# Four engines instead of one in the order of the program: a transformer layer on one core of Trainium2

## The chip, the cores and the metric

The kernel runs on one core of one Trainium2 chip. Times are device microseconds of that core. Five engines work at the same time, each through its own queue of instructions: TensorE (PE in the profile; PEld is its weight load), VectorE (DVE), ScalarE (ACT), GpSimd (POOL) and SyncE (SP), which here only issues DMAs. An instruction waits on semaphores until what it reads has been written and what it overwrites has been read; the instructions behind it in the same queue wait with it.

## The reference, cut to what matters

One layer over 4096 tokens of 256 features: attention with 16 heads of 16 features and a causal mask, and a feed-forward part with hidden size 1024, each followed by a residual and a layer norm.

```python
xn  = (x - mean) * rsqrt(var + 1e-5) * gamma + beta
q, k, v = split(xn @ w_qkv.T)                 # 16 heads of 16
attn = softmax(causal(q @ k.T / 4)) @ v       # 4096 x 4096 per head
x = layernorm(x + attn)
h = silu(x @ w1.T * s1) * (x @ w2.T * s2)     # 256 -> 1024
h = gelu(h @ h1.T * s_h1)                     # 1024 -> 1024
h = gelu(h @ h2.T * s_h2)                     # 1024 -> 1024
x = layernorm(x + h @ w3.T * s3)              # 1024 -> 256
```

Everything is float32. The kernel splits operands of products into a high and a low part of a rounded kind (`fp32r`, written `FR`) and adds the products, so that a product is two or three matmuls.

## The kernel before, in words

The tokens are cut into 8 blocks of 512. Three kinds of work are woven into one stream on TensorE.

**Projections** (`projections`, a generator). For each block: load x (`xb`, SP), layer norm (`norm_steps`: statistics `st` and `mv` on VectorE, L132 and L133; `ve` and `rs` on GpSimd, L137 and L138; `mr` on VectorE, L141; four applies on ScalarE, L145), transposes and `xn` (`front`, L221 and L222), the split into `xh` and `xl` (L227, L229); then the products for keys, queries and values, each copied out of PSUM as a high and a low part (`kh` L263, `kl` L265; values `vst` L287) and written to DRAM (`kaug`, `qaug`, `vaug`). From the second block on GpSimd issues those writes. Two buffers hold `xb`, two each `kh` and `kl`.

**Attention.** Blocks of queries are taken in the order `ORDER`, four heads at a time. `row_max` forms all scores of a query block once for their row maxima: for every 128 queries and two heads a score tile of two PSUM banks (L435, with the mask added on the diagonal by `pick` and `tri`, L442), reduced by VectorE into `mp` (L446), which GpSimd has set to a large negative value before (L426). `scores` forms the scores a second time, transposed and with the maximum subtracted in the product (L479), ScalarE takes the exponential (`p`, L483), GpSimd clears what lies over the diagonal (L486, an affine select), and `product` multiplies by the values into `opsum` (L497). The score tiles of both, the projections' outputs and the small transposes share three PSUM buffers with the tag `s`; transposes and feed-forward products share one buffer with the tag `m`.

**Feed-forward** (`feed`, a generator for each block; two may be under way). Weights are loaded by GpSimd's DMA queue into three buffers a slot (`wt`, L660) while the block runs. The tanh (L789) and two combinations (L790, L792) make the gated product; L834 copies the hidden products out; `gelu` (L743) changes ScalarE's table and takes four tiles at once; GpSimd splits the results into high and low parts (`act`, L738 and L739). Two output products (L854) are scaled by VectorE (`th`, L861) and added to the residual by GpSimd (L863), followed by the layer norm with the same steps and the store.

**What sets the order.** The Python code emits instructions in one order, the order of the program. The loop in `layer` emits up to three tiles of row maxima and scores and then calls `other`, which emits a piece of projections or feed-forward work and products by the values. Small work that waits for something is put off by hand: `defer` puts a step into a lane with a delay, and `chore`, called once by each `other`, takes at most one ripe step out of the lanes. Splits after a gelu, the residual and the steps of the layer norm go through these lanes.

From that list a scheduler makes each engine's queue, by its own estimate of when an instruction is ready. For TensorE it is held to the order of the program: `in_order` adds an edge from each instruction of an engine to the engine's next one, and is called for TensorE alone. The queues of VectorE, ScalarE, GpSimd and SP are the scheduler's, with one exception: exponentials and gelus are chained to one another on ScalarE (`chain("table")`). In the projections the first block's loads and statistics stand under a high priority.

The last block's feed-forward part runs alone at the end (`self.tail`). There GpSimd has no splits, VectorE makes them, and `inspect` (L714) compares every weight tile with a second, raw copy loaded by SP, and counts differences. At the very end a branch on that count chooses a general path, which is not taken with these inputs.

Of the kernel before, what the change touches and what calls it, by code (L numbers as in the profile page):

```python
# [21 lines left out]
NB = N // B  # L22
# [21 lines left out]
def tokens(ap):  # L44
    return ap.rearrange("(t p) e -> p t e", p=P)


class Layer:
# [13 lines left out]
    @contextmanager  # L62
    def in_order(self, *engines):

        block = self.nc.cur_bb.bb
        start = len(block.instructions)
        yield
        last = {}
        for i in block.instructions[start:]:
            if i.engine in engines:  # L70
                if i.engine in last:
                    self.after(i, last[i.engine])
                last[i.engine] = i.name
# [8 lines left out]
    def run(self):  # L82
        tc, nc, a = self.tc, self.nc, self.a
        with ExitStack() as ctx:
            dram = self.pool(ctx, "dram", space=DRAM)
            cst = self.pool(ctx, "cst")
            self.small = self.pool(ctx, "small", 4)
            self.qaug = [dram.tile([H, 48, B], F32, name=f"qaug{b}") for b in range(NB)]
            self.kaug = [dram.tile([H, KR, B], F32, name=f"kaug{b}") for b in range(NB)]
            self.vaug = [dram.tile([NQ, P, 4, 4, D + 1], F32, name=f"vaug{b}") for b in range(NB)]  # L90
            self.attn = [dram.tile([B, E], F32, name=f"attn{b}") for b in range(NB)]

            self.ident = cst.tile([P, P], F32, name="ident")
            make_identity(nc, self.ident)
            self.mhalf = cst.tile([P, 4], F32, name="mhalf")
            nc.gpsimd.memset(self.mhalf, -0.5)
            self.wbad = cst.tile([P, 22], F32, name="wbad")
            self.wseq = (
                [("glu", g, 0) for g in range(4)]
                + [(n, g, k) for n in ("h1T", "h2T") for g in range(4) for k in range(2)]  # L100
                + [("w3T", 0, k) for k in range(2)]
            )
            self.sc = {}
            for n in ("w1_s", "w2_s", "h1_s", "h2_s"):
                self.sc[n] = cst.tile([P, 8], F32, name=n)
            self.w1_half = cst.tile([P, 8], F32, name="w1_half")
            self.w12 = cst.tile([P, 8], F32, name="w12")
            self.s3 = cst.tile([P, E], F32, name="s3")

            with ExitStack() as fctx, self.in_order(mybir.EngineType.PE):  # L110
                self.layer(fctx)
            bad = self.verdict(cst)
            with tc.If(bad > 0), ExitStack() as gctx:
                self.general(gctx)
# [86 lines left out]
    def projections(self, ctx):  # L201

        nc, a, ps = self.nc, self.a, self.ps
        one = self.pool(ctx, "p1", side="right")
        wk = self.pool(ctx, "pw", 2, side="right")

        def norm(b):  # L210
            xb = wk.tile([P, 4, E], F32, name="xb")
            nc.sync.dma_start(xb, tokens(a["x"][b * B : (b + 1) * B]))
            self.layernorm(xb, xb)
            return xb

        def front(b, xb):
            xn = wk.tile([P, 2, B], F32, name="xn", bufs=1)
            for c in range(2):
                tp = ps.tile([P, B], F32, name="m", tag="m")
                for t in range(4):  # L220
                    nc.tensor.transpose(tp[:, t * P : (t + 1) * P], xb[:, t, c * P : (c + 1) * P], self.ident)  # L221
                nc.scalar.activation(  # L222
                    xn[:, c], tp, AF.Identity, bias=bet[:, c : c + 1], scale=gam[:, c : c + 1]
                )
                yield 4 * TRANSPOSE, True
            xh = wk.tile([P, 2, B], FR, name="xh")
            nc.vector.tensor_copy(xh, xn)  # L227
            xl = wk.tile([P, 2, B], FR, name="xl")
            nc.vector.tensor_tensor(xl, xn, xh.bitcast(F32), ALU.subtract)  # L229
            parts[b] = xh, xl  # L230

        w = one.tile([P, 2, 3 * E], F32, name="wqkv")
        nc.scalar.dma_start(w, a["wqkvT"].rearrange("(k p) f -> p k f", p=P))
        gam = one.tile([P, 2], F32, name="gam")
        nc.scalar.dma_start(gam, a["gamma"].rearrange("(c p) -> p c", p=P))
        bet = one.tile([P, 2], F32, name="bet")
        nc.scalar.dma_start(bet, a["beta"].rearrange("(c p) -> p c", p=P))
        parts = {}
        with self.tc.high_priority():
            xb = norm(0)  # L240
            yield from front(0, xb)
        xb = norm(1)
        wh = one.tile([P, 2, 3 * E], FR, name="wh")
        nc.vector.tensor_copy(wh, w)
        wl = one.tile([P, 2, 3 * E], FR, name="wl")
        nc.vector.tensor_tensor(wl, w, wh.bitcast(F32), ALU.subtract)
        ones = one.tile([32, B], F32, name="ones")
        nc.gpsimd.memset(ones, 1.0)
        vst = [one.tile([P, NQ, 4, 4, D + 1], F32, name=f"vst{i}") for i in range(2)]
        for v in vst:  # L250
            nc.gpsimd.memset(v, 1.0)
        for b in range(NB):
            xh, xl = parts.pop(b)
            prods = [(wh, xh, c) for c in range(2)] + [(wl, xh, c) for c in range(2)] + [(wh, xl, c) for c in range(2)]
            for off, dst, order in ((E, self.kaug, (0, 0, 1)), (0, self.qaug, (0, 1, 0))):
                kp = ps.tile([P, 2, B], F32, name="s", tag="s", bufs=3)
                for T in range(2):
                    for n, (wp, xp, c) in enumerate(prods):
                        nc.tensor.matmul(
                            kp[:, T], wp[:, c, off + T * P : off + (T + 1) * P], xp[:, c], start=n == 0, stop=n == 5  # L260
                        )
                kh = wk.tile([P, 2, B], FR, name="kh")
                nc.scalar.copy(kh, kp)  # L263
                kl = wk.tile([P, 2, B], FR, name="kl")
                nc.vector.tensor_tensor(kl, kp, kh.bitcast(F32), ALU.subtract)  # L265
                for n, (i, g) in enumerate(sorted((i, g) for g, i in enumerate(order))):
                    for T in range(2):
                        queues = (nc.scalar, nc.sync, nc.gpsimd) if b == 0 else (nc.gpsimd,)
                        queues[(2 * n + T) % len(queues)].dma_start(
                            dst[b][8 * T : 8 * T + 8, 16 * g : 16 * g + 16, :], (kh, kl)[i][:, T].bitcast(F32)  # L270
                        )
                yield 12 * MM, True
                if dst is self.kaug:
                    nc.sync.dma_start(self.kaug[b][:, 48:KR, :], ones)
                    if b + 1 < NB:
                        yield from front(b + 1, xb)
                        if b + 2 < NB:
                            xb = norm(b + 2)
            v = vst[b % 2]
            vps = ps.tile([P, 4, E], F32, name="s", tag="s", bufs=3)  # L280
            for t in range(4):
                for n, (wp, xp, c) in enumerate(prods):
                    nc.tensor.matmul(
                        vps[:, t], xp[:, c, t * P : (t + 1) * P], wp[:, c, 2 * E :], start=n == 0, stop=n == 5
                    )
            for t in range(4):
                nc.scalar.copy(v[:, :, t, :, 0:D], vps[:, t].rearrange("p (q h d) -> p q h d", q=NQ, d=D))  # L287
            nc.gpsimd.dma_start(
                self.vaug[b].rearrange("q p t h d -> p q (t h d)"), v.rearrange("p q t h d -> p q (t h d)")
            )  # L290
            self.projected = b
            yield 12 * MM, True
# [702 lines left out]
```

## Time and profile before

| | |
|---|---|
| median of 3 runs | 2544.71 us (2540.38 to 2558.79) |
| profiled execution | 2547.4 us, of it 2545.2 from the first to the last instruction |
| busy: PE, DVE, ACT, POOL | 2263.3, 1540.0, 1389.4, 706.4 us |
| granted TensorE clock, mean | 0.926 |
| DMA | 310.02 MB, mean 122 GB/s |

A busy time says what an engine worked in the span; a view by windows gives the same for a stretch of it, with the granted clock. In the waits, a line reads: who waited, for whom, how long in all, how often, and the longest. In the timeline, a line reads: start, duration, engine, line of the kernel, operation, tile written from tile read, shapes, count, and in brackets the idle time of the engine just before with what ended it. "SPq" and "ACTq" are DMA issues by those queues.

### The profile page before, as it was taken

Reading aid. Unit: us, or ns where it says so; the run is one execution under the profiler, and the core shown is the slowest. Engines: PE = TensorE matmul, PEld = TensorE weight load, DVE = VectorE, ACT = ScalarE, POOL = GpSimd, SP = SyncE. Lnnn points to the kernel's source line nnn. Section 1 sums busy time; section 2 is a strip of 40 time slices with the busy share of each in tenths; the row PEclk is TensorE's granted clock in tenths of the full one; section 3 lists DMA queues with packets and bytes.
Section 4 is the critical chain, followed back from the end, with each engine's and each line's share of the span. In section 5 each row is a group of like instructions: output and inputs, shape, how many; then the busy total and the mean of one; then the engine's idle time right before and its main releaser. Section 6 shows DMA issues by size and latency. Waiting matters only on the chain. (4 is left out here: it accounts for less than half of the span.)

```text
span 2545.2 us, 36334 instructions
## 1 busy us (share of the span) xinstructions
PE 2263.3 (89%) x13986; PEld 1218.5 (48%) x13986; DVE 1540.0 (61%) x1800; ACT 1389.4 (55%) x1695; POOL 706.4 (28%) x1021
## 2 busy tenths in 40 slices
PE   4777989999998989999998989889999999999776
PEld 3555445445445545544454534444455543445355
DVE  3544777675666576676755577556766468761164
ACT  3332645555665665556655656556655667566621
POOL 3333232341323142403304041232313132221311
PEclk8887879989999989999998989999999989999989
DMA  7766644536454435444444434435353543443365
GB/s 208 203 164 178 149 108 120 118 103 128 109 119 128 117 81 118 106 118 120 110 115 106 106 94 113 114 102 136 90 124 102 126 112 88 116 111 87 94 178 154
DMA packets 251795, 310.02 MB, mean 122 GB/s; under 512 B 41312, under 2 KB 179680, under 8 KB 251616
## 3 DMA queue, kind: packets, MB, share of 16 engines
q1 hardware_dynamic: 141904, 184.87, 25.8%
q0 software_dynamic: 108352, 120.91, 21.6%
q8 instruction: 113, 1.85, 0.3%
q10 hardware_dynamic: 1360, 1.84, 0.2%
q14 instruction: 66, 0.54, 0.1%
HBM read 268.45 MB, written 38.54 MB: 121 GB/s over the span
## 5 line engine op out<-in xcount | busy, mean ns | idle before, releaser
L446 DVE TENSOR_REDUCE mp<-s 128x2 f32<-128x1024 f32 (+3 forms) x1152 | 1270.0, 1132 | 587.3 <-PE s L435 438.7
L483 ACT ACTIVATE p<-s 128x1024 f32<-128x1024 f32 (+3 forms) x1152 | 1060.5, 954 | 704.5 <-PE s L479 694.2
L479 PE MATMUL s<-qt,sk 50*128 50x512 f32 (+3 forms) x2304 | 514.4, 453 | 88.5 <-DVE mp L446 46.5
L435 PE MATMUL s<-mk,qt 48*128 48x512 f32 (+3 forms) x2304 | 515.0, 448 | 71.9 <-DVE mp L446 30.0
L497 PE MATMUL opsum<-p,vk 128*17 128x512 f32 (+3 forms) x4608 | 559.5, 587 | 11.9 <-POOL p L486 11.3
L816 PE MATMUL m<-act,wt 128*128 128x512 f32 x1792 | 480.5, 411 | 1.2 <-issue 1.1
L479 PEld LDWEIGHTS s<-qt,sk 50*128 50x128 f32 x2304 | 223.4, 193 | 403.6 <-DVE mp L446 145.5
L435 PEld LDWEIGHTS s<-mk,qt 48*128 48x128 f32 x2304 | 230.5, 197 | 326.3 <-ACT p L483 148.8
L816 PEld LDWEIGHTS m<-act,wt 128*128 128x128 f32 x1792 | 324.1, 191 | 125.7 <-issue 55.3
L497 PEld LDWEIGHTS opsum<-p,vk 128*17 128x17 f32 x4608 | 97.8, 97 | 240.0 <-issue 208.9
L486 POOL TENSOR_SCALAR_AFFINE_SELECT p<-p 128x256 f32<-128x256 f32 x256 | 102.9, 411 | 297.0 <-ACT p L483 295.6
L660 POOL DMA_DIRECT2D wt<-h2T_in x64 | 48.6, 759 | 411.7 <-PE m L816 338.6
L660 POOL DMA_DIRECT2D wt<-h1T_in x64 | 49.3, 770 | 361.8 <-PE m L816 225.5
L739 POOL TENSOR_TENSOR act<-raw,act 128x512 fp32r<-128x512 f32 x112 | 140.3, 1272 | 0.0
L834 ACT ACTIVATE raw<-m,h_s 128x512 f32<-128x512 f32 x112 | 77.1, 689 | 111.3 <-PE m L816 111.3
L786 PE MATMUL m<-xh,wt 128*128 128x512 f32 x224 | 103.9, 464 | 15.7 <-DVE th L790 14.1
L442 PEld LDWEIGHTS s<-tri,pick 64*128 64x128 f32 x1024 | 98.6, 209 | 7.1
L786 PE MATMUL m<-xl,wt 128*128 128x512 f32 x224 | 91.6, 409 | 0.0
L442 PE MATMUL s<-tri,pick 64*128 64x128 f32 (+1 forms) x1024 | 90.0, 255 | 0.0
L738 POOL CAST act<-raw 128x512 fp32r<-128x512 f32 x112 | 65.3, 610 | 54.9 <-ACT raw L743 54.9
L816 PE MATMUL bank<-act,wt 128*128 128x512 f32 x256 | 65.2, 411 | 15.2 <-DMA wt<-h2T_in 6.7
L738 POOL CAST act<-th 128x512 fp32r<-128x512 f32 x56 | 34.5, 616 | 145.7 <-DVE th L792 145.6
(118 smaller groups left out, 1480.2 us busy)
## 6 DMA issues: line engine op xcount, KB each, us to landing
mk<-kaug SPq DMA_DIRECT2D x288, 200.0 KB
sk<-kaug SPq DMA_DIRECT2D x288, 200.0 KB
wt<-h1T_in POOLq DMA_DIRECT2D x64, 512.0 KB, 4.3
wt<-h2T_in POOLq DMA_DIRECT2D x64, 512.0 KB, 4.2
vk<-vaug SPq DMA_DIRECT2D x144, 136.0 KB
qt<-qaug SPq DMA_DIRECT2D x64, 192.0 KB
wt<-w1T_in POOLq DMA_DIRECT2D x34, 256.0 KB, 4.0
wt<-w2T_in POOLq DMA_DIRECT2D x34, 256.0 KB, 4.1
```

The costliest lines, as they stand in the source:

```text
L435: nc.tensor.matmul(m[:, e, :k1], qt[rows, r, t * P : (t + 1) * P], kt[rows, r, :k1], start=True, stop=kb != qb,)
L442: nc.tensor.matmul(m[:, e, k1 - P + half * i : k1], pick[rows, i], tri[rows, : P - half * i], start=False, stop=i == 1,)
L446: nc.vector.tensor_reduce(mp[:, r, :, t, kb], m[:, :, :k1], AX.X, ALU.max)
L479: nc.tensor.matmul(s[:, e, lo:], kt[rows, r, t * P : (t + 1) * P], qt[rows, r, lo:], start=True, stop=True)
L483: nc.scalar.activation(p[:, :, lo:], s[:, :, lo:], AF.Exp, scale=0.25)
L486: nc.gpsimd.affine_select(out=p[:, :, lo : lo + P], in_=p[:, :, lo : lo + P], compare_op=ALU.is_ge, fill=0.0, base=0, pattern=[[0, 2], [1, ...
L497: nc.tensor.matmul(opsum[32 * j : 32 * j + D + 1, lo:], vt[:, t, j], pt[j // 2][:, j % 2, lo:], start=first, stop=last,)
L660: self.nc.gpsimd.dma_start(dst, src)
L738: eng.tensor_copy(hi, src)
L739: eng.tensor_tensor(lo, src, hi.bitcast(F32), ALU.subtract)
L786: nc.tensor.matmul(s, wt[:, 2 * i + k, cols], x[:, k], start=k == n == 0, stop=k == n == 1)
L816: nc.tensor.matmul(s, wts[k // 4][:, k % 4, cols], x[:, k % 4], start=k == n == 0, stop=k == 7 and n == 1)
```

## The change

The order of the program becomes binding for VectorE, ScalarE and GpSimd too; instructions that issue DMAs are left out of it on every engine, so that the scheduler still places them. In the projections, the high priority of the first block goes. The load of a block's x and its layer norm, which `norm` emitted together, are pulled apart: `fetch` emits the load at the old place, and the layer norm comes later in the program, for the second block behind the split of the weights and the fills of `ones` and `vst`, for the later blocks between the key and query products and the value product.

```diff
@@ in_order
-            if i.engine in engines:
+            if i.engine in engines and "DMA" not in type(i).__name__:
@@ run
-            with ExitStack() as fctx, self.in_order(mybir.EngineType.PE):
+            own = mybir.EngineType
+            with ExitStack() as fctx, self.in_order(own.PE, own.DVE, own.Activation, own.Pool):
                 self.layer(fctx)
@@ projections
-        def norm(b):
+        def fetch(b):
             xb = wk.tile([P, 4, E], F32, name="xb")
             nc.sync.dma_start(xb, tokens(a["x"][b * B : (b + 1) * B]))
-            self.layernorm(xb, xb)
             return xb
...
-        with self.tc.high_priority():
-            xb = norm(0)
-            yield from front(0, xb)
-        xb = norm(1)
+        xb = fetch(0)
+        ahead = fetch(1)
+        self.layernorm(xb, xb)
+        yield from front(0, xb)
+        xb = ahead
         wh = one.tile([P, 2, 3 * E], FR, name="wh")
...
         for v in vst:
             nc.gpsimd.memset(v, 1.0)
+        self.layernorm(xb, xb)
         for b in range(NB):
...
                         if b + 2 < NB:
-                            xb = norm(b + 2)
+                            xb = fetch(b + 2)
+            if b + 2 < NB:
+                self.layernorm(xb, xb)
             v = vst[b % 2]
```

Lines of the changed kernel lie up to four higher than before: the row maxima at L450, the exponentials at L487.

## The prediction

> **What bounds the kernel now.** I read the page's busy table first, then the span cut into four stages, then the waits of VectorE (DVE) and TensorE (PE), then the timeline around the longest PE gaps.
>
> ```profile
> PE 2263.3 (89%) x13986; PEld 1218.5 (48%) x13986; DVE 1540.0 (61%) x1800; ACT 1389.4 (55%) x1695; POOL 706.4 (28%) x1021
> ...
> PEclk8887879989999989999998989999999989999989
> ```
>
> ```profile
> core 0: us, PE busy (x) PEld busy (x) DVE busy (x) ACT busy (x) POOL busy (x), PEclk, DMA share, GB/s
> 0.00:60.00 60.00, 26.25 (x121) 20.84 (x121) 22.28 (x56) 20.05 (x35) 20.85 (x46) 0.87 0.73 202
> 60.00:256.00 196.00, 144.02 (x895) 103.82 (x895) 95.74 (x152) 66.12 (x119) 74.86 (x136) 0.80 0.71 186
> 256.00:2368.00 2112.00, 1964.01 (x12345) 1006.82 (x12349) 1345.69 (x1443) 1248.63 (x1473) 568.60 (x790) 0.94 0.45 112
> 2368.00:2546.00 178.00, 128.97 (x630) 87.01 (x627) 76.23 (x149) 54.60 (x69) 42.12 (x50) 0.89 0.53 145
> ```
>
> PE sets the time in the long third stage: 1964 of 2112 us busy. It is idle 34 us in the first stage, 52 in the second, 148 in the third, 49 in the last. So what the other engines' order is worth must be read from those gaps. VectorE's waits tell why they arise:
>
> ```profile
> DVE st L132 <- POOL x L863: 38.4, 13, 8.5
> DVE st L132 <- DMA xb<-x_in: 26.4, 6, 6.7
> DVE st L132 <- POOL x L679: 26.0, 5, 9.1
> ```
>
> (total, times, longest). A statistics instruction stands in VectorE's queue before its input is ready, and the row maxima behind it, which free the score buffers, wait too. One such place:
>
> ```profile
> 1361.32 1.25 POOL L863 TENSOR_TENSOR x<-x,th 128x512 f32<-128x512 f32 x1
> 1362.54 0.40 POOL L486 TENSOR_SCALAR_AFFINE_SELECT p<-p 128x256 f32<-128x256 f32 x1
> 1362.61 0.75 DVE L132 BATCH_NORM_STATS2 st<-x 128x6 f32<-128x256 f32 x2 [8.44 <-POOL x L863]
> 1363.28 2.34 DVE L446 TENSOR_REDUCE mp<-s 128x2 f32<-128x1024 f32 x2
> 1364.54 0.80 PE L479 MATMUL s<-qt,sk 50*128 50x512 f32 x2 [7.94 <-DVE mp L446]
> ```
>
> VectorE sat 8.44 us before `st` until GpSimd (POOL) had added the residual; two row maxima, long ready, followed; PE lost 7.94 us. GpSimd was late because splits of the other block filled it without a break from 1349.4 to 1361.3.
>
> **The change, stage by stage.** No matmul is added or removed, and PE's own order is the same. The sum is made against the profiled execution: 2547.4 us, span 2545.2, and it lies 2.7 above the median of 2544.7.
>
> *Third stage, 256 to 2368: statistics, splits, selects.* In the order before, two of a feed-forward block's four statistics stand 0 to 2 row maxima after each of its two output products (L861); in the changed order all four stand 5 to 12 row maxima after the second, in each of the six blocks that end beside row maxima. One maximum takes 1.22 us, so they come 6 us or more later, against blocked times of up to 8.5. Splits were issued back to back (0.61 cast and 1.27 subtraction each; from 897.8 to 907.4 without a break, and PE waited 5.03 us for the select behind them); now selects come between. PE gaps over 1.2 us that these moves explain, in order of time: 2.03, 1.86, 4.72, 5.03, 7.94, 3.31, 5.28, 7.66, 4.48, together **42.3 us**. I take all as gone.
>
> Each gap is also followed by a stretch of granted clock 0.50. Eight such stretches belong to these gaps: 17.1, 6.8, 17.1, 13.7, 20.5, 10.2, 10.2, 6.8, in all 102.4 us, in which the windows view has PE busy 72.6. Here a rule is weighed. The Trainium skill, "TensorE: Matmul & The Clock Gate", its table of terms and "HAM oscillation", prices the penalty at throttled time times one minus the granted share: 102.4 x 0.5 = 51 us. But 30 of the 102 are the gaps themselves, which I have counted; by the row 72.6 x 0.5 = 36 is the most. Half of that ran beside VectorE working off its backlog (busy 49.6 of the 102), which limits PE at any clock. I take half of 36, **18 us**. By the rule the stage's gain would be 93, by the row 79, my value 60.
>
> Against it stand new waits. ScalarE's (ACT's) tanh at L789 and VectorE's L790 behind it now stand back to back with no row maximum between; 22 of them wait 24.4 us now, 1.1 each; were all 56 to wait it, VectorE loses 62 us more or less, of which PE sees what the three score buffers don't cover. VectorE is idle 766 us of this stage, so I take a fifth, **12 us** (ends 0 and 62). The 32 `mp` memsets (0.2 us each), which ran far ahead on GpSimd, now stand where a row-maximum step begins, on average 52 places later. In the changed order 13 follow a select, 9 a split, 5 a `rs`, none directly a weight trigger (10 did before); I cost them at nothing beyond the 12, cover being the two other score buffers, some 2.3 us. Third stage: -42 - 18 + 12 = **-48 us**, ends -79 and +20.
>
> *First stage, 0 to 60.* Without `vst`'s memset (1.01 us) between `ve` and `rs`, and without `wh` and `wl` (0.93 and 1.72 us) ahead of `mr`, the first apply starts some 2.5 us earlier. Those two casts then stand behind `xl`, so the first products start at about 18.7 instead of 19.2. Block 2's `xn` no longer waits behind block 3's apply (the 9.4 us PE gap to 45.1); block 2's own apply, now behind `kl` of the first queries, ends about 38.7, which makes PE's next product some 3.4 us earlier. But `pick`, `tri`, `opsum` and the first `mp` memsets, done by 17 us before, now come after block 1's 12 POOL triggers and the third block's `ve` and `rs` (1.3 us). Those triggers end at 60.5 now, about 57 then; with 1.3 and some 2.2 of memsets and copies the first row maximum can run at about 60.5 to 61, where it runs at 61.2. I take **0**, ends -4 and +4. SP's order changes little: the feed-forward's first two x loads go ahead of the eight `ones` loads, 0.5 MB each, landing long before use.
>
> *Second stage, 60 to 256: projections beside attention.* Gone: 3.83, 4.75 and 7.49 us, where PE waited for VectorE blocked in statistics, 16 us; 27.2 us at clock 0.50 follow them with PE busy 19.4, worth up to 10, I take 7. New: in six blocks the layernorm is issued in one piece. From the first `st`, VectorE needs 2.2 us, GpSimd 1.3 (0.27 and 1.05), and ScalarE holds its exponentials until then, and for four applies (2.4) after: about 6 us, of which the V products (2.8 us) and two buffers hide all but 2: 6 x 2 = 12. About five `mp` memsets stand behind six key or query triggers (0.6 us each), 1 us each: 5. -23 + 17 = **-6 us**, ends -23 and +18, because the DMA engines are 71% busy and some gaps wait for them.
>
> *Last stage.* The comparison of weights with their raw copy (L714, 1.22 us) moves behind the split of the even chunk, where it stood ahead of the product. A weight buffer is free only when PE and this comparison are both done with it; PE needs it until 1.9 us into the odd chunk, the comparison is now done 3.4 us into it, so the next `wt` trigger comes 1.5 us later. PE already waits for those transfers:
>
> ```profile
> PE bank L816 <- DMA wt<-h2T_in: 6.7, 4, 2.0
> PE bank L816 <- DMA wt<-h1T_in: 5.1, 4, 2.1
> ```
>
> This is where a rule speaks against the change: "DMA: Bandwidth & Descriptors", its rules for kernel authors, wants a DMA issued early and its semaphore waited on late. By it the 1.5 us is paid in all eight waits, 12 us; by the row, in which the DMA engines are 83% busy from 2453 to 2526 and the bandwidth is part of the limit, it could be 0. I take **7**. The last block's residual and statistics now follow the other block's `mr`: 0.4 us more. Together +7.
>
> **Sum:** 0 - 6 - 48 + 7 = -47; 2547.4 - 47 = 2500 in a profiled execution, and 2544.7 - 47 = **2498 us** in the median.
>
> **Rivals.** About 1%, 25 us, is what a measurement of this kernel can tell from no change.
> *Deeper:* all of the clock and no new waits: -79 - 23 + 7 = -95, 2450 us. For it: the gaps and slow stretches are in the rows. Against: some 83 us of the third stage's idle is in gaps under 1.2 us, which VectorE and ScalarE at 64% and 59% leave anyway.
> *Swallowed:* in strict order VectorE and ScalarE wait for one another at each tanh, `hl`, `xl` and reciprocal, which the old order filled with maxima: the 12 becomes 50, the second stage +0: 0 + 0 - 10 + 7 = -3, about 2540. For it: `hl` and `xl` stand 2.6 and 2.8 places earlier. Against: PE consumes in the same order, so who waits, waits for what PE needs next.
> *Slower, by the `mp` memsets:* a memset caught behind a blocked weight trigger holds the row maxima. A trigger waits 7.0 us for PE (715.4 in 102), plus 0.76 and 0.2, less 2.3 of cover: 5.7 each. From 8 of 32 the gain is eaten; with 16 it is +91 - 47 = +44, 2589 us. For it: 13 stand within four places behind a trigger. Against: none directly behind one.
> That the order isn't what it says is ruled out by the two programs' orders of instructions side by side.
>
> **Chances.** Forecast 0.46 (its own range 2475 to 2519), deeper 0.15, swallowed 0.25, slower 0.14. Faster: 0.46 + 0.15 = 0.61; within 1%: 0.25; slower 0.14. Leaving out a third of deeper and most of slower gives 2452 to 2566.
>
> **What would show it.** Right: `st` waits on L863 and L679 near 0; no PE gap over 4 us between 300 and 2370; PEclk of the third stage at 0.97 or more; PE waits for `wt` in the last stage at 17 to 24 us. Wrong: VectorE's first maximum waiting for the memset by more than 2 us each; `xb` applies with long idle before them and PE idle over 52 us from 60 to 256.

## The result: 0.5% faster, a gain of 64 us beside a loss of 50

The changed kernel takes 2537.89 us (median of 20 runs, 2529.82 to 2549.54), the kernel before 2551.14 in the same series (20 runs). The ratio is 0.9947, 95% interval 0.9927 to 0.9966: 13 us faster where 47 were forecast. The profiled execution spans 2530.6 us, before 2545.2. Its page, busy time of TensorE and granted clock in 40 slices:

```profile
PE 2259.3 (89%) x13986; PEld 1218.9 (48%) x13986; DVE 1546.9 (61%) x1800; ACT 1391.5 (55%) x1695; POOL 708.4 (28%) x1021
...
PEclk8778989979998989999999999999999999999787
```

Between the 17th slice and the last three, the clock row of before has three slices at 8 (the prediction shows the row); now there is none. The last three read 787 where 989 stood. The totals hide this. Since TensorE's order is the same in both, the span can be cut where the same work has been done. I take the start of two row-maximum reductions, numbers 96 and 1151 counted from 0 among the 1184 reductions into or from `mp` (the expectations below call them the 96th and the last, though 32 more follow the second). The windows between and behind these marks, first of the changed kernel:

```profile
core 0: us, PE busy (x) PEld busy (x) DVE busy (x) ACT busy (x) POOL busy (x), PEclk, DMA share, GB/s
293.10:2191.20 1898.10, 1802.76 (x11480) 926.14 (x11473) 1285.96 (x1380) 1158.26 (x1366) 531.89 (x734) 0.96 0.46 115
2191.20:2531.00 339.80, 249.61 (x1257) 152.14 (x1253) 115.00 (x186) 126.00 (x150) 69.14 (x86) 0.85 0.40 109
```

The same work in the kernel before:

```profile
293.90:2255.50 1961.60, 1821.09 (x11480) 935.87 (x11477) 1285.17 (x1380) 1155.27 (x1363) 529.67 (x732) 0.95 0.44 111
2255.50:2546.00 290.50, 237.71 (x1257) 142.75 (x1253) 111.97 (x186) 125.97 (x150) 68.61 (x86) 0.91 0.47 127
```

The counts of TensorE (11480, 1257) agree, so the pieces may be subtracted. Up to mark 96 the kernels differ by 0.8 us, between the marks the changed one is 63.5 us shorter, and behind mark 1151 it is 49.7 us longer (339.4 to its own end against 289.8). In the middle TensorE's idle time fell from 140.5 to 95.3 us and its busy time from 1821.1 to 1802.8. At the end its idle time rose and its clock fell from 0.91 to 0.85.

VectorE's waits in the changed kernel (total, times, longest) show which waits went:

```profile
DVE mp L450 <- POOL mp L430: 21.8, 9, 4.6
...
DVE st L133 <- DMA xb<-x_in: 6.4, 1, 6.4
DVE st L133 <- POOL x L867: 1.0, 1, 1.0
```

Statistics waited 38.4 us for the residual's addition and 26.0 for the attention's; 1.0 is left of both. TensorE's waits show where the end is longer:

```profile
PE bank L820 <- DMA wt<-h1T_in: 24.8, 5, 6.4
PE bank L820 <- DMA wt<-h2T_in: 21.2, 4, 5.9
...
PE bank L858 <- DMA wt<-w3T_in: 4.7, 1, 4.7
```

Before, these weight waits were 5.1, 6.7 and 1.9 us. One pair of hidden chunks in the last stage shows how 2 us of waiting became 6. The timeline of the changed kernel (start, duration, engine, line; in brackets the idle time before):

```profile
2388.00 8.88 PE L820 MATMUL bank<-act,wt 128*128 128x512 f32 x32 [2.91 <-DMA wt<-h1T_in]
...
2391.47 0.69 ACT L832 ACTIVATE th<-bank,h_s 128x512 f32<-128x512 f32 x1 [11.14 <-PE bank L820]
2392.20 0.43 DVE L742 CAST act<-th 128x512 fp32r<-128x512 f32 x1 [3.71 <-ACT th L832]
...
2393.27 1.22 DVE L718 SCALAR_TENSOR_TENSOR raw<-raw,wt 128x1024 f32<-128x1024 f32 x1
...
2395.03 0.74 POOL L664 DMA_DIRECT2D wt<-h1T_in  x1 [5.25 <-DVE raw L718]
...
2396.18 0.74 POOL L664 DMA_DIRECT2D wt<-h1T_in  x1 [0.41 <-issue]
...
2403.29 1.22 PE L820 MATMUL bank<-act,wt 128*128 128x512 f32 x2 [6.41 <-DMA wt<-h1T_in]
```

And the same place in the kernel before:

```profile
2459.60 1.23 DVE L714 SCALAR_TENSOR_TENSOR raw<-raw,wt 128x1024 f32<-128x1024 f32 x1 [0.49 <-DMA wt<-h1T_in]
...
2459.62 7.55 PE L816 MATMUL bank<-act,wt 128*128 128x512 f32 x32 [0.95 <-DMA wt<-h1T_in]
...
2461.77 0.69 ACT L828 ACTIVATE th<-bank,h_s 128x512 f32<-128x512 f32 x1 [5.01 <-PE bank L816]
...
2463.84 0.95 POOL L660 DMA_DIRECT2D wt<-h1T_in  x1 [6.77 <-PE bank L816]
...
2465.66 0.74 POOL L660 DMA_DIRECT2D wt<-h1T_in  x1 [0.87 <-PE bank L816]
```

Before, the comparison runs the moment its weight has landed, beside TensorE's first products with it, and what frees the buffer is TensorE. In the changed kernel it stands behind the even chunk's gelu and split, and the trigger's releaser is `raw L718`. That holds for eight triggers (before, for none):

```profile
POOL wt L664 <- DVE raw L718: 90.9, 8, 14.5
```

Measured from the even chunk's gelu, the first trigger comes after 3.56 us instead of 2.07, 1.5 us later. From then to TensorE's next start 8.3 us pass instead of 5.4 (to 2469.28 in the trace of before). The copies for the comparison are set off by the same comparisons:

```profile
2394.52 0.37 SPq L717 DMA_DIRECT2D raw<-h1T_in  x1
...
2395.67 0.37 SPq L717 DMA_DIRECT2D raw<-h1T_in  x1
```

So four transfers of 0.5 MB start within 1.7 us. In the pair of before they are spread over 4.8 us (copies at 2460.86 and 2464.18). Over seven pairs of chunks (first to fifteenth gelu of the two hidden layers) a pair takes 105.56 / 7 = 15.1 us, before 68.77 / 7 = 9.8.

### The profile page after: what moved, and what is told of

Its sections match the earlier page's. It is cut to its first block, busy times and chain, and to the rows that moved or that the text cites. A ratio compares the mean times of both kernels' runs of the same rounds, so it can differ in the third digit from the quotient of the medians.

```text
span 2530.6 us, 36361 instructions
## 1 busy us (share of the span) xinstructions
PE 2259.3 (89%) x13986; PEld 1218.9 (48%) x13986; DVE 1546.9 (61%) x1800; ACT 1391.5 (55%) x1695; POOL 708.4 (28%) x1021
## 5 line engine op out<-in xcount | busy, mean ns | idle before, releaser
L450 DVE TENSOR_REDUCE mp<-s 128x2 f32<-128x1024 f32 (+3 forms) x1152 | 1264.8, 1132 | 549.3 <-PE s L439 393.3
L487 ACT ACTIVATE p<-s 128x1024 f32<-128x1024 f32 (+3 forms) x1152 | 1062.8, 954 | 664.9 <-PE s L483 648.2
L439 PE MATMUL s<-mk,qt 48*128 48x512 f32 (+3 forms) x2304 | 509.8, 444 | 56.2 <-DVE mp L450 17.8
L501 PE MATMUL opsum<-p,vk 128*17 128x512 f32 (+3 forms) x4608 | 552.6, 581 | 2.4 <-POOL p L490 1.4
L820 PE MATMUL m<-act,wt 128*128 128x512 f32 x1792 | 473.3, 406 | 0.7 <-DVE xl L773 0.7
L501 PEld LDWEIGHTS opsum<-p,vk 128*17 128x17 f32 x4608 | 97.4, 97 | 230.6 <-issue 211.4
L490 POOL TENSOR_SCALAR_AFFINE_SELECT p<-p 128x256 f32<-128x256 f32 x256 | 102.1, 408 | 286.6 <-ACT p L487 281.4
L820 PE MATMUL bank<-act,wt 128*128 128x512 f32 x256 | 76.8, 467 | 46.0 <-DMA wt<-h1T_in 24.8
L790 PE MATMUL m<-xh,wt 128*128 128x512 f32 x224 | 104.1, 465 | 12.8 <-DVE th L794 10.2
L820 PEld LDWEIGHTS bank<-act,wt 128*128 128x128 f32 x256 | 58.8, 234 | 64.1 <-DMA wt<-h1T_in 19.7
```

Source lines behind the costliest of these rows:

```text
L439: nc.tensor.matmul(m[:, e, :k1], qt[rows, r, t * P : (t + 1) * P], kt[rows, r, :k1], start=True, stop=kb != qb,)
L450: nc.vector.tensor_reduce(mp[:, r, :, t, kb], m[:, :, :k1], AX.X, ALU.max)
L487: nc.scalar.activation(p[:, :, lo:], s[:, :, lo:], AF.Exp, scale=0.25)
L490: nc.gpsimd.affine_select(out=p[:, :, lo : lo + P], in_=p[:, :, lo : lo + P], compare_op=ALU.is_ge, fill=0.0, base=0, pattern=[[0, 2], [1, ...
L501: nc.tensor.matmul(opsum[32 * j : 32 * j + D + 1, lo:], vt[:, t, j], pt[j // 2][:, j % 2, lo:], start=first, stop=last,)
L790: nc.tensor.matmul(s, wt[:, 2 * i + k, cols], x[:, k], start=k == n == 0, stop=k == n == 1)
```

## The experiments

All times by mark are of profiled executions, the medians and ratios of the runs beside the kernel before on the same chip (its median was 2548.75 to 2554.18 us in those series).

| | to mark 96 | 96 to 1151 | 1151 to end | median | ratio, interval |
|---|---|---|---|---|---|
| before | 293.9 | 1961.6 | 289.8 | 2551.14 | |
| changed | 293.1 | 1898.1 | 339.4 | 2537.89 | 0.9947 (0.9927 to 0.9966) |
| early comparison | 290.5 | 1902.0 | 293.8 | 2489.53 | 0.9804 (0.9744 to 0.9864) |
| order only | 322.1 | 1909.9 | 345.5 | 2569.95 | 1.0074 (1.0042 to 1.0105) |
| by hand only | 294.5 | 1961.4 | 288.1 | 2546.15 | 0.9991 (0.9969 to 1.0013) |
| statistics loose | 292.3 | 1910.8 | 336.5 | 2550.28 | 0.9988 (0.9966 to 1.0010) |
| GpSimd ordered | 294.4 | 1939.7 | 290.4 | 2528.20 | 0.9906 (0.9886 to 0.9925) |
| VectorE ordered | 300.2 | 1913.9 | 343.3 | 2559.21 | 1.0031 (1.0009 to 1.0053) |
| ScalarE ordered | 282.4 | 1957.3 | 289.0 | 2535.82 | 0.9938 (0.9915 to 0.9960) |
| no raw copies | 297.0 | 1898.6 | 304.7 | 2502.63 | 0.9816 (0.9759 to 0.9872) |
| VectorE, not statistics | 301.5 | 1955.8 | 339.2 | 2594.41 | 1.0167 (1.0109 to 1.0225) |
| late start | 281.4 | 1904.1 | 296.2 | 2490.14 | 0.9767 (0.9703 to 0.9831) |
| memsets loose | 301.5 | 1891.0 | 292.2 | 2477.64 | 0.9707 (0.9655 to 0.9758) |
| last stage ordered | 291.0 | 1962.6 | 342.4 | 2601.43 | 1.0212 (1.0156 to 1.0267) |

A mark is read from a single execution. Three of the kernels have the same program up to the last stage (changed, early comparison, no raw copies); they reach mark 96 at 290.5 to 297.0 us and take 1898.1 to 1902.0 between the marks. So differences of some 7 us in the first column and 4 us in the second can be chance.

**Early comparison.** The changed kernel with the comparisons of a pair emitted ahead of the even chunk's gelu and split.

```diff
                 if self.tail:
-                    if c % 2:
+                    if c % 2 == 0:
                         for k in range(2):
                             self.inspect(g + k, wts[k])
```

> The changed kernel with one edit in the last stage: the two weight comparisons of a pair of chunks (L718) are emitted ahead of the even chunk's gelu and split instead of behind it. Theory A (late comparisons hold the weight buffers, so the weight transfers and the copies for the comparison all start together at the end of a pair and DMA idles before): the pair of chunks, 15.4 us long in the changed kernel, goes back to about 9.3 us, PE's waits for wt from 51 to about 15 us, half clock in the last stage from 70.7 to about 45; all in all 2538 - 48 = 2490 us, ratio to before 0.975 to 0.979. Rival B (the order of POOL's triggers or bandwidth sets the pair's length): pairs stay at 14 us or more, and the time within 8 us of 2538, ratio 0.993 to 0.997.

Measured: 2489.53 us. The last stage falls from 339.4 to 293.8 us and a pair to 9.1. TensorE's waits for weights:

```profile
PE bank L820 <- DMA wt<-h1T_in: 11.4, 6, 3.6
PE bank L820 <- DMA wt<-h2T_in: 4.6, 4, 1.7
```

Theory A holds: one move of two instructions carries nearly all of the loss, and without it the order gives 2%. What is left of the loss is a wait of TensorE for the last comparison, 4.6 us, which this edit does not move.

**Last stage ordered.** The reverse: the kernel before, with VectorE's order binding only behind the point where the last block's feed-forward begins.

```diff
         self.tail = True
+        self.mark = len(nc.cur_bb.bb.instructions)
@@ in_order
-        for i in block.instructions[start:]:
-            if i.engine in engines:
+        dve = mybir.EngineType.DVE
+        for n, i in enumerate(block.instructions):
+            if n < (self.mark if i.engine == dve else start):
+                continue
+            if i.engine in engines + (dve,):
```

> The kernel before with one part of the change alone: VectorE's order binding in the last stage only, nothing else. Theory A (the place of the comparisons is the whole loss there): up to the last row maximum as before, the last stage 40 to 52 us longer, in all 2591 to 2604 us, ratio 1.016 to 1.021. Rival B (the loss needs GpSimd's or ScalarE's order as well): within 12 us of before.

Measured: 2601.43 us, the last stage 52.6 longer (just above the range) and the rest within 3. Theory A again, this time without any other part of the change.

**No raw copies.** What makes the landing long? The changed kernel without the loads of the raw copies, the comparison reading the weight tile twice.

```diff
-        for dst, src in self.sources(j, raw):
-            nc.sync.dma_start(dst, src)
         nc.vector.scalar_tensor_tensor(
-            raw, raw, 1.0, wt.bitcast(F32), ...
+            raw, wt.bitcast(F32), 1.0, wt.bitcast(F32), ...
```

> The changed kernel without the loads of the raw weight copies in the last stage (L717); the comparison reads the weight tile against itself, with the same VectorE work at the same place, so that no difference could be found. A pair of chunks took 15.4 us in the changed kernel, 9.25 before: the trigger of a weight load comes 2.7 us later after the pair's start, and trigger to landing takes 8.1 instead of 5.0 us. Theory A (the copies, set off at the same moment by the same comparison, make the landing long): landing at 5 us or less, a pair at 10.5 to 12.5 us, the last stage 25 to 40 us shorter, in all 2498 to 2513 us, ratio 0.979 to 0.985. Rival B (weights landing late only through the late trigger and the slower clock): landing at 7 us or more, a pair at 14 us or more, in all 2528 or more.

Measured: 2502.63 us, a pair at 72.34 / 7 = 10.3 us, just under the range. From the tile view of the weights' triggers, in the changed kernel (last stage):

```profile
DMA to landing us min/median/max: 4.1/8.0/8.7
```

and here:

```profile
DMA to landing us min/median/max: 3.3/4.1/5.4
```

(before: median 5.0). Theory A holds. With the comparison at its late place but no copies beside the weights, 34.7 of the 49.7 us are gone. In the changed kernel the DMA engines were busy 53% of the time from 2370 to 2500, in the kernel before 76% from 2437 to 2526: they waited, and then had two pairs of transfers at once. The amount alone is not the cause: the early comparison moves the same copies, and its weights land after a median of 5.0 us. From 2397 to 2403 us the trace of the changed kernel has packets of both queues, 929 of the weights' and 630 of the copies'. This agrees with the Trainium skill, "DMA: Bandwidth & Descriptors", section "Queues, rings and completion order", which says that a DMA engine takes turns between its queues packet by packet. Then a weight and a copy started together can both land late. The trace does not show the turns of a single DMA engine.

**Order only** and **by hand only.** The two parts of the change, each alone.

```diff
 order only: the kernel before, with
+            if i.engine in engines and "DMA" not in type(i).__name__:
+            with ExitStack() as fctx, self.in_order(own.PE, own.DVE, own.Activation, own.Pool):
 by hand only: the changed kernel, with
+            with ExitStack() as fctx, self.in_order(own.PE):
```

> The kernel before with the binding order for the four engines, without the placement by hand in the projections. Theory A (the order alone makes the third stage's gain, 64 us from 300 to 2310, and the last stage's loss of 50; the placement by hand repairs what the order would cost in the projections): third stage 60 to 70 us shorter than before, last stage 45 to 55 longer, and the time up to the 96th row maximum 10 to 30 us later than in the changed kernel, in all 2548 to 2568 us, ratio 0.999 to 1.007. Rival B (the placement is of no use, or part of the third stage's gain is its): up to the 96th maximum no later than the changed kernel, in all 2530 to 2545, ratio under 0.998, or a third stage that gains under 40 us.

> The placement by hand in the projections alone, with TensorE's order only, as before. Theory A (gain and loss are both of the order): third and last stage within 10 us of before, and so the whole, 2551 plus or minus 12 us, ratio 0.995 to 1.005. Rival B (the placement gives part of it): over 12 us faster than before, ratio under 0.995, gained before the 96th row maximum.

Measured: 2569.95 and 2546.15 us. The order alone has a gain in the middle (51.7, less than expected) and the loss at the end (55.7), and is 28.2 us late at mark 96. The placement by hand alone changes nothing that can be measured. It is worth 29 us where the order is binding and nothing where it is not. Both speak for theory A, though order only lies 2 us above its range and its gain in the middle 8 below the one expected.

**One engine's order at a time**, with the placement by hand.

```diff
-            with ... self.in_order(own.PE, own.DVE, own.Activation, own.Pool):
+            with ... self.in_order(own.PE, own.Pool):        # GpSimd ordered
+            with ... self.in_order(own.PE, own.DVE):         # VectorE ordered
+            with ... self.in_order(own.PE, own.Activation):  # ScalarE ordered
```

> The changed kernel with the binding order for TensorE and GpSimd only; VectorE's and ScalarE's queues are the scheduler's again, the placement by hand stays. Theory A (GpSimd's order makes most of the third stage's gain, because the residual's addition and the selects no longer stand behind a block's run of splits, and VectorE's order makes the last stage's loss): third stage, from the 96th to the last row maximum, 40 to 60 us shorter than before, last stage within 10 us of before, in all 2490 to 2512 us, ratio 0.976 to 0.985. Rival B (VectorE's order makes the gain, with the statistics and all else that it moves): third stage under 25 us shorter, in all 2525 to 2550.

> The changed kernel with the binding order for TensorE and VectorE only. Theory A: third stage 5 to 25 us shorter than before, last stage 45 to 55 us longer, in all 2570 to 2595 us, ratio 1.008 to 1.018. Rival B: third stage over 40 us shorter, in all under 2560.

> The changed kernel with the binding order for TensorE and ScalarE only. Theory A: within 12 us of the placement by hand alone (2546), every stage within 10 us of before. Rival C (ScalarE's order makes the gain, since exponentials no longer stand behind a copy or an apply that waits): third stage over 25 us shorter, in all under 2525.

Measured: 2528.20, 2559.21 and 2535.82 us. My theory A, that GpSimd's order makes most of the gain, falls: in the middle GpSimd's gives 21.9 us, VectorE's 47.7, ScalarE's 4.3, which can be chance. VectorE's also makes the whole loss at the end. ScalarE's order is 11.5 us early at mark 96, which neither theory had. Up to there TensorE is as busy as with the placement by hand alone (203.0 and 202.7 us), so waits went; no run looked for the cause.

**Statistics loose** and **VectorE, not statistics.** Which VectorE moves count? Statistics (`st`, `mv`) are left out of the binding order, once with all engines ordered, once with TensorE and VectorE only. The scheduler then puts them back to 0 to 2 row maxima behind an output product.

```diff
                 nc.vector.bn_aggr(mv[:, t], st)
+                self.loose |= {i.name for i in nc.cur_bb.bb.instructions[-2:]}
@@ in_order
-            ... and "DMA" not in type(i).__name__:
+            ... and "DMA" not in type(i).__name__ and i.name not in self.loose:
```

> The changed kernel with the statistics of all layer norms (st and mv, L133 and L134) left out of VectorE's binding order; the scheduler then puts two of a feed-forward block's four statistics again 0 to 2 row maxima behind each output product, as before. Theory A (blocked statistics made the kernel before slow in the third stage, as the prediction has it): waits of st for the residual's addition on GpSimd come back, 25 to 60 us in all, with PE gaps of 3 to 8 us at the same places, and the third stage loses 30 to 55 of its 64 us; in all 2570 to 2592 us, ratio 1.007 to 1.016. Rival B (the gain is from other moves: selects between splits, row maxima that no longer stand behind something else): within 10 us of 2538, ratio 0.991 to 0.999.

> The changed kernel with the binding order for TensorE and VectorE only, and the statistics st and mv left out of it, so that they stand early again. VectorE's order alone shortened the stretch from the 96th to the last row maximum by 47.6 us, with statistics left out but GpSimd ordered it was 50.7. Theory A (VectorE's part is the statistics' place, as the prediction has it; GpSimd's order is a second cure for the same waits, by bringing the residual's addition in time): that stretch gains under 15 us, waits of st for the addition at 30 us or more; in all 2585 us or more. Rival B (the statistics are a small part, other VectorE moves count): the stretch gains over 30 us, in all under 2575.

The first came out between its theories: 2550.28 us, 12.7 of the 63.5 us of the middle lost. The second bears out theory A: 2594.41 us, and VectorE's gain in the middle is down from 47.7 to 5.8. VectorE's waits tell the two apart, first with all engines ordered:

```profile
DVE st L134 <- POOL x L869: 11.4, 11, 2.1
```

then with GpSimd's queue left to the scheduler:

```profile
DVE st L134 <- POOL x L869: 37.0, 12, 8.7
```

The statistics stand early in both. The two differ in GpSimd's and in ScalarE's order, and the waits show what this changes: how late GpSimd's addition is. An early statistics instruction waits 2.1 us at most where the addition comes in time, and up to 8.7 where it is behind another block's splits (in the second, they fill GpSimd for more than 10 us before the longest wait ends). Moving the statistics back cures it, and so does GpSimd's order; done together the two cures overlap. They don't account for all. GpSimd ordered has `st` waits as short:

```profile
DVE st L133 <- POOL x L867: 14.2, 13, 2.1
```

Yet its middle is 28.9 us longer than that of statistics loose. Which other moves make that up, I did not separate.

**Late start.** The early comparison, with VectorE's and GpSimd's order binding only behind the projections.

```diff
             yield 12 * MM, True
+        self.mark = len(nc.cur_bb.bb.instructions)
@@ in_order
+        early = mybir.EngineType.PE, mybir.EngineType.Activation
+        for n, i in enumerate(block.instructions):
+            if n < (start if i.engine in early else self.mark):
+                continue
```

> The early comparison in the last stage (2489.5 us), and VectorE's and GpSimd's order binding only from the end of the projections on; TensorE's and ScalarE's from the start. With ScalarE's order alone the 96th row maximum ran 11 us earlier than in the changed kernel. Theory A (what the projections win or lose at the 96th maximum is kept to the end): 6 to 14 us under the early comparison, 2476 to 2484 us, ratio 0.970 to 0.975. Rival B (it is given back later, as the 7.7 us of the first row maximum were): within 5 us of 2489.

Measured: 2490.14 us, against 2489.53, with ratios whose intervals overlap. In the profiled executions it is 9.1 us ahead of the early comparison at mark 96 and still 7.1 at mark 1151, as theory A wants. The median lies in rival B's range, but with four runs each it can't tell the two apart. Unclear.

**Memsets loose.** The early comparison, with the memset of `mp` left out of GpSimd's order.

```diff
             nc.gpsimd.memset(mp, NEG)
+            self.loose.add(nc.cur_bb.bb.instructions[-1].name)
```

> The early comparison in the last stage, with the memsets of mp (L430) left out of GpSimd's order, so that they run far ahead. In the changed kernel the row maxima wait 21.8 us for them in 9 places, 4.6 at most, 13.6 of it before 260 us. Theory A (the score buffers hide most of it): within 6 us of 2489.5, no wait for the memset left. Rival B (the prediction's slower rival in small: each such wait is TensorE's too): 12 to 22 us faster, 2468 to 2478.

Measured: 2477.64 us, no wait for the memset left. It is the fastest median, 12 us under the early comparison, but from another series, and the intervals of the two ratios just overlap. In the profiled executions both reach mark 1151 at the same time, 2192.5 us, but the one profiled here was the slowest of its four runs, 9 us above their median. So the median speaks for rival B, the trace weakly for A; it stays open. This version and the early comparison both beat the kernel before by 2 to 3% and the changed kernel too.

## Why the prediction was wrong in size

Stage by stage the profiled execution measured -0.8 - 63.5 + 49.7 = -14.6 us, where 0 - 6 - 48 + 7 = -47 was forecast.

**The step that failed is the last stage's +7.** It measured +49.7. The mechanism was named, the weight trigger behind the comparison, and the lateness of 1.5 us was right to a tenth. The sum was not: TensorE's waits for weights were forecast at 17 to 24 us and came to 46.0 in the two hidden layers and 4.7 behind them. I multiplied 1.5 by the waits and took half, because the DMA engines were 83% busy. That reasoning ran the wrong way. The rule on issuing a DMA early, weighed there, would have paid 12; it was nearer, and still too low by four times. A pair is a closed loop (trigger, landing, TensorE and comparison, trigger), and the loop grew by 5.3 us: 1.5 for the trigger, 3.0 for the landing (8.0 for 5.0), and the rest, 0.8, beside a slower TensorE. Each of these ten waits in the changed kernel (2.9 to 6.4 us) has a stretch of 3.4 to 10.2 us at a granted clock of 0.50 beside it or within 1.2 us behind it. The nine of before (at most 2.1 us) have one, of 3.4. Seven pairs make 36.8 us. Another 4.9 lie ahead of the first gelu, and 8.0 behind the last pair, where the wait for the third kind of weights and a 4.6 us wait for the last comparison stand. I had counted where `wt` triggers go and forgotten that the same comparison frees the copies' buffers.

**Third stage, -48.** Measured -63.5. Gaps: -42.3 forecast, TensorE's idle time -45.2 measured. Clock: -18 forecast, TensorE's busy time -18.3 measured; time at half clock between the marks fell from 211.4 to 139.9 us, for which the rule of throttled time would have paid 36 us. TensorE's busy time in those stretches fell by 40.9 us, and half of that, 20.5, is near what came. New waits: +12 forecast, none seen. They came, but not for TensorE: VectorE waits 52.9 us for the tanh in 45 places (24.4 in 22 before), while TensorE's waits for `th` of the gated products went from 15.3 to 12.3 us. Longest TensorE gap between 300 us and mark 1151: 2.02 us, as forecast (those of 6.26 and 11.38 us at 2317 and 2356 belong to the last stage and are in the kernel before too). The granted clock reached 0.96, not 0.97.

The reading of the gaps held, and the statistics' place is VectorE's part of the gain. But that it is the early place that costs was half the story: with GpSimd in order it cost 12.7 us.

**First and second stage, -6.** Measured -0.8 at mark 96. The first row maximum was forecast for 60.5 to 61 us and ran at 69.0. I looked at GpSimd's triggers and took SP's order as little changed. In the trace SP issues the first queries' low part at 46.40 (41.76 before), behind an `mk` load that is itself late (46.02 for 40.70), and their `qt` load at 61.42 (48.08 before). TensorE waits 13.8 us for that load. No run isolates this, and by mark 96 it is made good. The sign of a wrong second stage did not come: TensorE is idle 51.9 us from 60 to 256.

**The rivals.** "Swallowed" gave 2540, close to what came, but by new waits in the middle that did not exist. "Slower by the `mp` memsets": its sign appeared (nine waits, 2.4 us each), its price did not: what is left open above is some 12 us.

## What to carry to other kernels

Before an order is made binding, look for every reader that frees a buffer, checks and copies included, and put it where its data arrives; its place sets when the next transfer starts. Price a later trigger as part of the whole loop, with all transfers that the same release sets off, and not as its lateness alone. When two engines' orders cure the same wait, measure each alone: their gains don't add.

## What the runs showed of the hardware

A 0.5 MB weight transfer took 4.1 us from trigger to landing with no copies beside it, 5.0 with the copies spread over the pair, and 8.0 with both copies and both weights started within 1.7 us. All three are medians of the same kind of transfer, and the mean load of the DMA engines was lower in the last case (53%) than in the second (76%).
